# One full reading of x in another order of tiles, and four constants loaded through another queue

## The chip, the core and the metric

The kernel runs on one core of one Trainium2 chip. Its engines work side by side, each on its own list of instructions in order: TensorE (PE, with its weight loads as PEld), VectorE (DVE), ScalarE (ACT), GpSimd (POOL) and SyncE (SP). SP, ACT and POOL also issue DMA transfers, which sixteen DMA engines carry out between HBM and the chip's memory (SBUF). An instruction starts when those ahead of it on its engine have started and the semaphores that it waits for have been raised. The metric is the device time of one execution in microseconds; lower is better.

## The reference, cut to what matters

Four layers are applied in turn to an image x of 256 x 256 pixels with 128 channels in float32, each in the form `x = x + layer(gn(x))`: an attention along the rows, a recurrence in the Fourier domain, a triangle product, and a 3 x 3 convolution. Each begins with a group norm over the whole image:

```python
def _gn(v, G=32, eps=1e-5):
    B_, H_, W_, C_ = v.shape
    g = v.reshape(B_, H_, W_, G, C_ // G)
    m = jnp.mean(g, axis=(1, 2, 4), keepdims=True)
    s = jnp.var(g, axis=(1, 2, 4), keepdims=True)
    return ((g - m) / jnp.sqrt(s + eps)).reshape(v.shape)

x = x + _L0_conv_ref(_gn(x), ...)
x = x + _L1_conv_ref(_gn(x), ...)
x = x + _L2_conv_ref(_gn(x), ...)
x = x + _L3_conv_ref(_gn(x), ...)
```

The mean and variance of x for the first group norm need a reading of all of x before the first layer can start. The change lies in that reading.

## The kernel before

**The reading of x.** `statistics` (L194) takes x as 32 tiles of 2048 pixels, each `[128, 2, 1024]` in float32, 1 MB, loaded by one DMA that SP issues (L236). Seven tiles, 0 to 6, are loaded into buffers of their own, `kept` (L349), because the pass that follows starts with them and so needn't read them again. The other 25 go through the three buffers of `xin` (L235): a load can be issued only when VectorE has read the tile that was in its buffer three loads earlier. The order of the tiles is written out in `order` (L229): first 7 to 31, last the kept ones.

For each half of a tile VectorE subtracts a shift, the values of the first pixel, into `xs` (L239, the line L217 of the profile); ScalarE squares it into `sqx` (L242, shown as L54); and TensorE adds up both over the pixels in `acc` (L225, shown as L60). `xs` has three buffers, and these three operations are kept in the order of the program.

**What runs beside it.** `constants` (L156) loads four tables of 64 KB through SP at the very start: `ident`, `cmat`, `omat` and `g4`. Then SP loads `row` and `shc`, the shift in two layouts, and from `row` TensorE and VectorE make `sh`. `attention_weights` (L271) loads weights through ScalarE's queue and prepares them with small operations on VectorE and TensorE; these stand in the engines' lists among the subtractions of the first tiles. One of its results passes through ScalarE (`terms`) before VectorE forms `tot`.

`kernel_rows` (L165) computes H, the rows of a spectrum that the second layer uses. It loads its taps `ka` through GpSimd's queue and its table `tu` through SP; then sixteen times, after tiles 4, 5, 7, 8 and so on up to 26 in order of reading, TensorE forms `ph` and ScalarE copies it into H (L188, shown as L178). After the eighth and after the sixteenth copy GpSimd's queue writes H to HBM in four DMAs of 224 KB (L191), each of 14 rows of 16 KB.

**What follows.** When `acc` is complete, VectorE copies it to `accs` (L256); a chain of small operations gives mean and variance, `group_affine` (L75) turns them into scale and shift with `g4`, and `centering` (L129) uses `cmat`. Then the first pass of the attention transposes tile by tile (`turn`, with `ident`), starting with the kept tiles, and loads tile 7 and on once more. SP's list holds, between the loads of the reading and those of this pass, 25 small loads of weights for later layers.

A Tile framework places the semaphores. The DMAs of SP and ACT share eight of them in turn, and GpSimd's eight others; a DMA whose semaphore is still awaited from an earlier transfer waits for that one. Where nothing pins an instruction, a scheduler decides its place on its engine.

The lines shown in the profile are those of the innermost statement, so `load` appears as L70, `mm` as L60 and `act` as L54.

Of the kernel before, what the change touches and what calls it, by code (L numbers as in the profile page):

```python
# [30 lines left out]
class Kernel:  # L31
# [33 lines left out]
        self.nc.sync.dma_start(t, src.rearrange("(c o) -> c o", o=1))  # L65
        return t

    def load(self, pool, src, name):
        t = pool.tile(list(src.shape), F32, name=name)
        self.nc.sync.dma_start(t, src)  # L70
        return t


# [81 lines left out]

    def constants(self, pool):  # L156
        nc = self.nc
        self.ident = self.load(pool, self.i["c_ident"], "ident")
        self.cmat = self.load(pool, self.i["c_center"], "cmat")
        self.omat = self.load(pool, self.i["c_mean"], "omat")  # L160
        self.g4 = self.load(pool, self.i["c_group4"], "g4")
        self.eps = pool.tile([P, 1], F32, name="eps")
        nc.vector.memset(self.eps, LN_EPS)

# [29 lines left out]
    def statistics(self, wp, weights, HD_, kept, src):  # L194

        nc, I = self.nc, self.i
        V = nc.vector
        x = I["x"].rearrange("b h w c -> (b h w) c")  # L200
        NM, KEPT = NPIX // 2048, len(kept)
        mv = wp.tile([P, 2], F32, name="mvx")
        with ExitStack() as c:
            sp = c.enter_context(self.pool(name="sp", bufs=1))
            io = c.enter_context(self.pool(name="p0", bufs=3))
            ps = c.enter_context(self.pool(name="p0s", bufs=1, space=PSUM))
            row = sp.tile([1, P], F32, name="row")
            nc.sync.dma_start(row, x[0:1])
            shc = self.column(sp, x[0:1].rearrange("o c -> (o c)"), "shc")
            ones = sp.tile([P, P], F32, name="ones0")  # L210
            V.memset(ones, 1.0)
            psh = ps.tile([P, 4, P], F32, name="psh", tag="ph", bufs=2)
            self.mm(psh[:, 0], ones[0:1], row)
            sh = sp.tile([P, P], F32, name="sh")
            V.tensor_copy(sh, psh[:, 0])
            acc = ps.tile([P, 512], F32, name="acc")
            pin = lambda f: lambda *a, **k: self.tc.keep_in_program_order(f(*a, **k))  # L217
            last, count = None, [0, 0]

            def add_up(*pair):  # L220
                for h in range(2):
                    for j, t in enumerate(pair):
                        if t is not None:
                            o = 64 * j + 32 * h
                            pin(self.mm)(acc[o:o + 32], ones[:, :32], t[:, h * 512:(h + 1) * 512],  # L225
                                    start=count[j] < 2, stop=count[j] >= 4 * NM - 2)
                            count[j] += 1

            order = list(range(KEPT, NM)) + list(range(KEPT))  # L229
            spectrum, made = None, 0  # L230
            for n, m in enumerate(order):
                if m < KEPT:
                    xin = kept[m]
                else:
                    xin = io.tile([P, 2, 1024], F32, name="xin", bufs=3)  # L235
                nc.sync.dma_start(xin, src(m))  # L236
                for b in range(2):
                    xs = io.tile([P, 1024], F32, name="xs")
                    pin(V.tensor_tensor)(xs.rearrange("p (t c) -> p t c", t=8), xin[:, b].rearrange("p (t c) -> p t c", t=8),  # L239
                                    sh.unsqueeze(1).to_broadcast([P, 8, P]), ALU.subtract)  # L240
                    sq = io.tile([P, 1024], F32, name="sqx")
                    pin(self.act)(sq, xs, AF.Square)  # L242

                    add_up(xs, last)
                    last = sq
                if n == 1:
                    spectrum = self.kernel_rows(sp, ps, HD_)
                    next(weights)
                elif n == 9:
                    weights = next(weights)  # L250
                elif n >= 4 and n % 3 and made < 16:
                    spectrum(made)
                    made += 1
            add_up(None, last)
            accs = sp.tile([P, 512], F32, name="accs")
            V.tensor_copy(accs, acc)  # L256
            sel = sp.tile([P, 2], F32, name="sel")
            V.memset(sel, 0.0)
            V.memset(sel[:64, 0:1], 1.0 / 32 / NPIX)
            V.memset(sel[64:, 1:2], 1.0 / 32 / NPIX)  # L260
            pm = ps.tile([P, 2], F32, name="pmx")
            for t in range(4):
                self.mm(pm, accs[:, t * P:(t + 1) * P], sel, start=t == 0, stop=t == 3)
            V.tensor_copy(mv, pm)
            e = sp.tile([P, 1], F32, name="ex")
            V.tensor_tensor(e, mv[:, 0:1], mv[:, 0:1], ALU.mult)
            V.tensor_tensor(mv[:, 1:2], mv[:, 1:2], e, ALU.subtract)
            V.tensor_tensor(mv[:, 0:1], mv[:, 0:1], shc, ALU.add)
        return mv, weights

    def attention_weights(self, wp):  # L271
# [4 lines left out]
        def load(src, name):  # L276
            t = wp.tile(list(src.shape), F32, name=name)
            nc.scalar.dma_start(t, src)
            return t

        lns, lnb = (load(I["L0_conv_ln_" + n].rearrange("(c o) -> c o", o=1), "ln" + n[0]) for n in ("scale", "bias"))
        w, wb, raws = {}, {}, {nm: load(I["L0_conv_W" + nm], "raw" + nm) for nm in "qkvgb"}
        wo = {"f": load(I["L0_conv_Wo"], "wo"), "h": wp.tile([P, P], F32, name="woh")}
        m32 = load(self.i["c_block32"], "m32")
        yield
# [1248 lines left out]
def arrays_of(inputs):  # L1534


    arrays = constants()
    for name, a in inputs.items():
        a = np.asarray(a)
        if name in _RENAMED:  # L1540
            if name == "L3_conv_kernel":
                a = a.reshape(9, P, P).transpose(2, 0, 1)
            else:
                a = a.T
            name = _RENAMED[name]
        arrays[name] = np.ascontiguousarray(a)


    taps = np.zeros((2, 3 * KS, HC, 32), np.float32)
    for n, m in enumerate("AB"):  # L1550
        re, im = (arrays.pop(f"L1_conv_{m}_{y}").transpose(1, 0, 2) for y in ("real", "imag"))
        for p0, q0, a in ((0, 0, re), (0, KS, im), (KS, 0, im), (2 * KS, KS, re)):
            taps[n, p0:p0 + KS, :, q0:q0 + KS] = a
    arrays["L1_taps"] = taps
    for g in "fid":
        arrays["L1_b" + g] = np.ascontiguousarray(np.tile(arrays.pop("L1_conv_b" + g).reshape(2, HC).T, (2, 1)))
    return arrays
# [16 lines left out]
```

## Time and profile before

| what | us |
|---|---|
| median of three runs | 5099.39 (5096.98 to 5099.84) |
| the profiled execution, its own time | 5096.92 |
| its span, first to last instruction | 5095.1 |
| TensorE busy in it | 4938.7 (97%) |
| first subtraction of the reading starts | 15.29 |
| last subtraction ends | 123.7 |
| `accs` copied out | 126.03 |
| first transposes of the pass that follows | 131.9 |

In a line of the timeline the first number is the start in microseconds from the start of the span, the second the time that it took, then engine, line, operation, what it writes and reads, and how many of them the line puts together. In brackets stands how long the engine was idle before it, and what released it. In a line of the windows stand the stretch, its length, then busy time of PE, PEld, DVE, ACT and POOL with their counts, the granted clock of TensorE, the busy share of the DMA engines and the GB/s that they moved. In a line of the queues stand packets, MB and the share of the time of 16 DMA engines; q1 is that of SP, q0 that of GpSimd.

### The profile page before, as it was taken

Reading aid. Unit: us, or ns where it says so; the run is one execution under the profiler, and the core shown is the slowest. Engines: PE = TensorE matmul, PEld = TensorE weight load, DVE = VectorE, ACT = ScalarE, POOL = GpSimd, SP = SyncE. Lnnn points to the kernel's source line nnn. Section 1 sums busy time; section 2 is a strip of 40 time slices with the busy share of each in tenths; the row PEclk is TensorE's granted clock in tenths of the full one; section 3 lists DMA queues with packets and bytes.
Section 4 is the critical chain, followed back from the end, with each engine's and each line's share of the span. In section 5 each row is a group of like instructions: output and inputs, shape, how many; then the busy total and the mean of one; then the engine's idle time right before and its main releaser. Section 6 shows DMA issues by size and latency. Waiting matters only on the chain. (4 is left out here: it accounts for less than half of the span.)

```text
span 5095.1 us, 78580 instructions
## 1 busy us (share of the span) xinstructions
PE 4938.7 (97%) x31357; PEld 2699.4 (53%) x31357; DVE 4100.7 (80%) x4797; ACT 3497.2 (69%) x4948; POOL 406.9 (8%) x592
## 2 busy tenths in 40 slices
PE   8999999999999899999999999899999999989999
PEld 2444555555555333333333333229999953349999
DVE  6666999999999799999999999775333537779886
ACT  6445888888888899999999999453333357762110
POOL 0331000000000000000000000240111010000000
PEclk9999999999999899999999999999999999999999
DMA  8894222222222222222222221588666778865432
GB/s 289 291 338 173 88 84 80 88 81 82 84 81 82 65 70 66 74 64 76 64 74 66 72 68 61 215 324 308 235 230 243 252 286 321 322 230 181 141 122 67
DMA packets 204461, 781.66 MB, mean 153 GB/s; under 512 B 56278, under 2 KB 59628, under 8 KB 154788
## 3 DMA queue, kind: packets, MB, share of 16 engines
q1 hardware_dynamic: 146638, 505.57, 29.6%
q0 software_dynamic: 56160, 270.64, 14.7%
q8 instruction: 250, 4.10, 0.3%
q14 instruction: 117, 0.96, 0.1%
q10 hardware_dynamic: 1296, 0.40, 0.0%
HBM read 505.18 MB, written 271.32 MB: 152 GB/s over the span
## 5 line engine op out<-in xcount | busy, mean ns | idle before, releaser
L565 DVE TENSOR_TENSOR e<-sc,bT 128x1024 f32<-128x1024 f32 x512 | 603.1, 1220 | 51.3 <-PE sc L60 50.4
L54 ACT ACTIVATE e<-e 128x1024 f32<-128x1024 f32 x512 | 540.3, 1055 | 63.1 <-DVE e L565 53.9
L1066 DVE TENSOR_TENSOR LR<-z,sg 128x512 f32<-128x512 f32 x256 | 268.6, 1049 | 363.5 <-ACT sg L54 363.5
L60 PE MATMUL m<-U,v 128*128 128x128 f32 x4608 | 516.9, 276 | 6.7 <-DVE v L1413 6.7
L60 PEld LDWEIGHTS m<-U,v 128*128 128x128 f32 x4608 | 516.8, 193 | 6.7 <-DVE v L1413 6.7
L60 PEld LDWEIGHTS z<-wf,zt 128*128 128x128 f32 x4096 | 460.0, 193 | 2.9 <-DVE zn L1066 2.7
L60 PE MATMUL z<-wf,zt 128*128 128x128 f32 x4096 | 460.2, 276 | 1.3 <-DVE zn L1066 1.3
L54 ACT ACTIVATE sg<-z 128x512 f32<-128x512 f32 x256 | 153.0, 597 | 308.8 <-PE z L60 308.8
L54 ACT ACTIVATE sq<-zs 128x1024 f32<-128x1024 f32 x192 | 202.4, 1054 | 196.3 <-DVE zs L374 156.9
L565 DVE TENSOR_TENSOR ks<-e 128x1024 f32<-128x1024 f32 x256 | 300.9, 1217 | 0.0
L60 PE MATMUL sc<-tq,tk 32*128 32x256 f32 x4096 | 297.7, 402 | 3.2 <-DVE e L565 2.3
L60 PEld LDWEIGHTS sc<-tq,tk 32*128 32x128 f32 x4096 | 186.9, 185 | 160.5 <-issue 97.1
L60 PE MATMUL nd<-e,tv 128*32 128x256 f32 x4096 | 271.7, 383 | 0.0
L54 ACT ACTIVATE dn<-dn 128x512 f32<-128x512 f32 x384 | 241.7, 629 | 14.2 <-DVE dn L565 3.4
L60 PE MATMUL av<-y,ident 128*128 128x512 f32 x384 | 191.3, 607 | 44.8 <-DVE y L903 44.8
L60 PE MATMUL po<-LR 128*128 128x256 f32 x1024 | 222.2, 380 | 7.0 <-DVE LR L1066 7.0
L1450 ACT COPY m4s<-m 128x512 f32<-128x512 f32 x32 | 18.7, 585 | 286.1 <-PE m L60 286.1
L60 PEld LDWEIGHTS po<-LR 128*128 128x128 f32 x1024 | 194.1, 190 | 34.2 <-DVE LR L1066 7.7
L60 PE MATMUL bx<-p,ident 128*128 128x512 f32 x384 | 193.3, 612 | 0.0
L54 ACT ACTIVATE o<-po 128x256 f32<-128x256 f32 x256 | 84.3, 381 | 145.3 <-issue 109.4
L60 PEld LDWEIGHTS nd<-e,tv 128*32 128x32 f32 x4096 | 120.2, 110 | 108.9 <-issue 42.9
L54 ACT ACTIVATE xp<-xr,ab 128x1536 f32<-128x1536 f32 (+1 forms) x48 | 76.9, 1653 | 137.6 <-DVE tf L1425 126.7
(364 smaller groups left out, 10354.7 us busy)
## 6 DMA issues: line engine op xcount, KB each, us to landing
zt<-znT SPq DMA_DIRECT2D x128, 1024.0 KB
znT<-zn POOLq DMA_DIRECT2D x64, 1024.0 KB, 5.2
xin<-x2T SPq DMA_DIRECT2D x64, 1024.0 KB
xin<-in_x_dram SPq DMA_DIRECT2D x50, 1024.0 KB
xr<-x3T SPq DMA_DIRECT2D x46, 768.0 KB
xT<-xo POOLq DMA_DIRECT2D x32, 1024.0 KB, 9.4
xr<-xT SPq DMA_DIRECT2D x64, 512.0 KB
zn<-znT SPq DMA_DIRECT2D x64, 512.0 KB
```

The lines of the kernel that those rows point to most:

```text
L54: return self.nc.scalar.activation(out, in_, func, bias=bias, scale=scale, **kw)
L60: return self.nc.tensor.matmul(out, lhsT, rhs, start=start, stop=stop)
L565: pin = lambda f: lambda *a, **k: tc.keep_in_program_order(f(*a, **k))
L1066: pin = lambda f: lambda *a, **k: tc.keep_in_program_order(f(*a, **k))
L1450: nc.scalar.copy(m4, m[4])
```

## The change

The reading takes the tiles in the order of their numbers, so the seven kept tiles come first and the 25 that go through `xin` after them. The four constants are loaded through GpSimd's queue instead of SP's, ahead of the taps.

```diff
-    def load(self, pool, src, name):
+    def load(self, pool, src, name, queue=None):
         t = pool.tile(list(src.shape), F32, name=name)
-        self.nc.sync.dma_start(t, src)
+        (queue or self.nc.sync).dma_start(t, src)
         return t
...
-        self.ident = self.load(pool, self.i["c_ident"], "ident")
-        self.cmat = self.load(pool, self.i["c_center"], "cmat")
-        self.omat = self.load(pool, self.i["c_mean"], "omat")
-        self.g4 = self.load(pool, self.i["c_group4"], "g4")
+        self.ident = self.load(pool, self.i["c_ident"], queue=nc.gpsimd, name="ident")
+        self.cmat = self.load(pool, self.i["c_center"], queue=nc.gpsimd, name="cmat")
+        self.omat = self.load(pool, self.i["c_mean"], queue=nc.gpsimd, name="omat")
+        self.g4 = self.load(pool, self.i["c_group4"], queue=nc.gpsimd, name="g4")
...
-            order = list(range(KEPT, NM)) + list(range(KEPT))
+
             spectrum, made = None, 0
-            for n, m in enumerate(order):
+            for n in range(NM):
+                m = n
                 if m < KEPT:
                     xin = kept[m]
                 else:
```

In the built program the order of instructions differs only in this stage. On SP, `row` and `shc` come first, then the loads of the seven kept tiles (with `tu` after the second), then those of the 25 others. On GpSimd the four constants stand ahead of the taps. On VectorE `sh` is made first, and the preparation of the weights is spread among the subtractions of the first six tiles. On TensorE and ScalarE the same operations stand in a slightly different order in the first tiles.

## The prediction

> **What bounds the kernel now.** I first read the whole span, then the stage that the diff touches, then what waits for what inside it.
>
> ```profile
> span 5095.1 us, 78580 instructions
> PE 4938.7 (97%) x31357; PEld 2699.4 (53%) x31357; DVE 4100.7 (80%) x4797; ACT 3497.2 (69%) x4948; POOL 406.9 (8%) x592
> ```
>
> TensorE is busy nearly everywhere, so a change in the first stage moves all later work as a block: what the stage gains or loses is the whole effect. The reading of x (L236) ends where `accs` is copied out, at 126.03 us. That is 2.5% of the span. The copies of the weight table and the first transposes follow by 132 us.
>
> The pace of that stage is in the timeline of ScalarE:
>
> ```profile
> 58.49 1.03 ACT L178 COPY H<-ph 128x512 f32<-128x512 f32 x1 [1.23 <-PE ph L60]
> ...
> 68.53 1.02 ACT L178 COPY H<-ph 128x512 f32<-128x512 f32 x1 [1.23 <-PE ph L60]
> ...
> 74.47 1.04 ACT L178 COPY H<-ph 128x512 f32<-128x512 f32 x1 [1.23 <-PE ph L60]
> ...
> 78.54 1.02 ACT L178 COPY H<-ph 128x512 f32<-128x512 f32 x1 [1.23 <-PE ph L60]
> ...
> 89.63 1.06 ACT L178 COPY H<-ph 128x512 f32<-128x512 f32 x1 [2.40 <-PE ph L60]
> ...
> 113.74 1.02 ACT L178 COPY H<-ph 128x512 f32<-128x512 f32 x1 [1.23 <-PE ph L60]
> 114.56 10.31 ACT L54 ACTIVATE sqx<-xs 128x1024 f32<-128x1024 f32 x10
> ```
>
> Every three tiles bring two copies of H, and the same one of the two comes back after 10.03 us (58.49, 68.53, 78.54): 3.34 us a tile, set by ScalarE's squares, its copies and its two waits for PE. Once in the stage the beat breaks: the successor of 74.47 was due at 84.5 and comes at 89.63. After 113.74 there are no more copies, and a tile takes about 2.35 us. VectorE's timeline says why it breaks, and when the stage starts and ends:
>
> ```profile
> 15.29 2.35 DVE L217 TENSOR_TENSOR xs<-xin,sh 128x1024 f32<-128x1024 f32 x2
> ...
> 24.76 2.36 DVE L217 TENSOR_TENSOR xs<-xin,sh 128x1024 f32<-128x1024 f32 x2 [0.34 <-PE ptot L533]
> ...
> 27.59 4.61 DVE L217 TENSOR_TENSOR xs<-xin,sh 128x1024 f32<-128x1024 f32 x4
> ...
> 76.40 1.23 DVE L217 TENSOR_TENSOR xs<-xin,sh 128x1024 f32<-128x1024 f32 x1 [1.28 <-ACT sqx L54]
> 83.72 2.36 DVE L217 TENSOR_TENSOR xs<-xin,sh 128x1024 f32<-128x1024 f32 x2 [6.09 <-DMA xin<-in_x_dram]
> ...
> 111.59 2.40 DVE L217 TENSOR_TENSOR xs<-kept,sh 128x1024 f32<-128x1024 f32 x2 [1.29 <-ACT sqx L54]
> 115.64 8.08 DVE L217 TENSOR_TENSOR xs<-kept,sh 128x1024 f32<-128x1024 f32 x7 [1.65 <-ACT sqx L54]
> 126.03 0.69 DVE L256 COPY accs<-acc 128x512 f32<-128x512 f32 x1 [2.30 <-PE acc L60]
> ```
>
> The 6.09 us wait at 83.72 is for a tile of x. Just before it POOL has written H to HBM (first of two times):
>
> ```profile
> 69.84 2.00 POOL L191 DMA_DIRECT2D HD<-H  x4 [67.31 <-ACT H L178]
> 115.05 2.00 POOL L191 DMA_DIRECT2D HD<-H  x4 [43.20 <-ACT H L178]
> ```
>
> The queues of 66 to 90 us and the windows show the price of that write:
>
> ```profile
> q1 hardware_dynamic: 1561, 6.05, 68.5%
> q0 software_dynamic: 128, 0.92, 22.7%
> ```
>
> ```profile
> 100.00:114.00 14.00, 13.47 (x116) 3.21 (x112) 9.78 (x9) 10.31 (x12) 0.00 (x0) 1.00 1.02 409
> 72.00:82.00 10.00, 9.18 (x78) 2.01 (x70) 4.34 (x4) 6.89 (x8) 0.00 (x0) 1.00 0.97 243
> ```
>
> The write moves 0.92 MB for 22.7% of 24 us on 16 engines, 95 us of engine time per MB; reads of x cost 43.5. While it runs (72 to 82 us) all queues together move 2.43 MB, so x gets 1.51 MB, 1.44 tiles in 10 us; undisturbed (100 to 114 us, 409 GB/s) a tile of 1.05 MB takes 2.56 us. **The second write starts at 115.05, in the last tiles.** There it hurts nobody today: those are the kept tiles, each with a buffer of its own, and SP has issued all seven by 100 us.
>
> **What the Trainium skill says.** "DMA: Bandwidth & Descriptors", section "Queues, rings and completion order": each DMA engine goes round-robin among the queues that have work, packet by packet, so H and x share the same engines; the 243 against 409 GB/s agrees. The same page, "Why a DMA increments its semaphore by 16 and not by 1": the engine count divides the slowest dimension, so H's 14 rows would go to 14 engines in few large pieces; the dear engine time above fits, the split itself no view shows. "Anatomy of one DMA — SWDGE (gpsimd) path": about 2.0 us fixed and bytes/436e3, so about 4.4 us for one tile alone (an estimate from the page). I use 5 us from issue to use: the wait at 36.00 and the like (0.2 to 1.3 us) in the three-buffer loop allow that little slack. "TensorE: Matmul & The Clock Gate", Part 1, gives a half clock after an idle window; the 0.50 windows at 28 and 132 us agree.
>
> **The change part by part.**
>
> (1) Constants to GpSimd's queue. SP loses four issues of 0.40 to 0.43 us, POOL gains four of about 0.6 (its taps' issues take 0.62). SP's first tile is now issued third, near 2 us instead of 5.41, since it also no longer waits for lanes that the constants held. POOL's taps come 4 x 0.6 = 2.4 us later; they are first read near 30 us, nothing. `ident` is first read by VectorE near 13 us and `cmat`, `g4` after 128 us: nothing, unless ident took over 10 us.
>
> (2) Tiles 0 to 6 first. Ten buffers (seven kept, three of `xin`) take loads without waiting for VectorE. Today SP's fourth tile waits until 17.67 for VectorE, and in 16 to 18 us the DMA moves only 35 GB/s. In the built program the first subtraction now stands just behind `grq`, where nine small operations preceded it after `wo` landed: today `woh` at 12.47, `xs` at 15.29, 2.8 us. And the fifth tile's subtraction stands ahead of `tot`, which covers today's 2.22 us wait for ScalarE's `terms`. If `wo` lands at 11 to 13 us (12.4 today; it is issued earlier, against more traffic), the five first tiles, with their 17 us of VectorE work less the 0.9 us put behind them, end at 27.5 to 29.5 instead of 32.2: a gain of 2.7 to 4.7. I take 3.5; the bounds are 0 (weights come late by what was won) and 6.
>
> (3) The middle. From the sixth tile on ScalarE paces, so the lead of the loads isn't cashed: nothing. At the first write of H the tile that comes late (the 20th) can't be issued before the 17th's buffer is free (71.7 us), with or without a lead; the write is on by 71.9. So the 5.1 us of the broken beat (89.63 less 84.5) stay. I take 0.3 gained; bounds 0 and 5.
>
> (4) The end. The last tiles go through three buffers: tile n+3 is issued when VectorE has done with n. In today's clock, the 30th tile (of 32) is issued at 109.1 and is in time; the 31st when the 28th is done, at 112.8; its transfer starts near 114.5, behind the 30th, and has some 0.4 tile left when the write of H takes hold near 116. The 32nd is issued when the 29th is done, at 116.9. So 1.4 tiles pass beside the write at 1.44 tiles in 10 us: until about 125.6, and 1.2 more until it is seen, 126.8. Its two subtractions end at 129.2; today VectorE ends at 123.7. Loss 5.5; bounds 1 (the write starts late enough for the 31st to pass) and 8.
>
> (5) Behind the stage. SP's 25 loads of later weights and the loads of tile 7 on come some 10 us later; tile 7 is transposed from 195 us on, and today its load is issued at 134.69, so 55 us cover it. The pass after has a beat of 9.54 us of PE with and without loads of x: nothing.
>
> Sum: -3.5 - 0.3 + 5.5 = +1.7 us. The profiled execution took 5096.92 (span 5095.1 and 1.8 around it), so 5098.6 by that clock; it lies 2.5 under the median of 5099.39, which gives 5101 for the median.
>
> **The rivals.** *The last loads escape the write of H*: for it, only 0.4 tile of the 31st stands in its way; against it, the 32nd can't be issued earlier. Then the end costs 1 to 2 us and the change nets -2: 5097. *The early lead covers the first write too*: head -6 and the 5.1 us of the broken beat gone, end at 1: about -10, 5089. Against it, the buffer rule in (3). *Slower, crowded head*: the tiles of x, from 2 us on, share the engines with the six weight loads of 64 KB on ScalarE's queue, for which VectorE waits in order before it subtracts anything. Price: 8 packets of each on an engine, each behind a packet of x (4 KB at 43.5 us per MB, 0.18 us), 1.4 us a load, six in a row 8.6. Then the first subtraction comes near 21 instead of 15.29 and with the end's 5.5 the sum is about +11: 5111. It decides once `wo` lands after about 18 us. For it: today rawq takes 4.1 us and wo 5.2, which is such sharing already; against it, the weights are issued earlier as well. *Nothing moves*: the pace is ScalarE's, head and end both hide: 5099.
>
> **How the numbers follow.** Main case 0.62; loads escape 0.16; nothing moves 0.07; both stalls gone 0.05; crowded head 0.10. 0.2% is 10 us, about what this measurement can tell from no change. Main, escape and nothing stay within it (0.85, and 0.01 from the edge of the others), the fourth is faster (0.04), the fifth slower. Range: the main case is +1.7 with -4 to +6 from its bounds; with part of the others 5095 to 5108.
>
> **What would show it.** Right: first subtraction near 12 us and the fifth tile done by 29; a wait of some 5 us for `xin` still in the middle; at the end waits of VectorE for `xin` of 5 us together, where today it has none; `accs` near 127.5. Wrong: `wo` after 18 us; no wait for `xin` in the last ten microseconds of the reading; a shift that arises after 140 us.

## The result, and the profile after

| | before | after |
|---|---|---|
| median of 20 runs each, us | 5098.59 (5093.95 to 5100.64) | 5103.61 (5101.17 to 5110.10) |
| ratio, 95% interval | | 1.0014 [1.0008, 1.0020] |
| the profiled execution, its own time | 5096.92 | 5101.69 |
| its span | 5095.1 | 5099.5 |
| first subtraction starts | 15.29 | 13.84 |
| first copy of H | 34.41 | 31.77 |
| last copy of H | 113.74 | 111.19 |
| `accs` copied out | 126.03 | 132.08 |

The changed kernel is slower by some 0.14%, which its interval tells from nothing, and which lies within the 0.2% that the forecast called no change. The stage of the reading is 6.05 us longer in the profile. The table splits it: 2.64 us are won before the first copy of H; at the last copy 2.55 of them are left, so the middle gave back 0.09; and between the last copy and `accs` the kernel before took 12.29 us, the changed one 20.89. This last difference, 8.6 us, is called *the end* below; it is worked out for each kernel as `accs` less the last copy of H less 12.29.

VectorE's timeline of the changed kernel shows the head, the break in the middle and the end:

```profile
13.84 2.35 DVE L217 TENSOR_TENSOR xs<-kept,sh 128x1024 f32<-128x1024 f32 x2
...
26.72 2.36 DVE L217 TENSOR_TENSOR xs<-kept,sh 128x1024 f32<-128x1024 f32 x2
...
81.16 2.36 DVE L217 TENSOR_TENSOR xs<-xin,sh 128x1024 f32<-128x1024 f32 x2 [6.17 <-DMA xin<-in_x_dram]
...
113.10 5.81 DVE L217 TENSOR_TENSOR xs<-xin,sh 128x1024 f32<-128x1024 f32 x5 [1.65 <-ACT sqx L54]
126.63 2.36 DVE L217 TENSOR_TENSOR xs<-xin,sh 128x1024 f32<-128x1024 f32 x2 [7.72 <-DMA xin<-in_x_dram]
132.08 0.69 DVE L257 COPY accs<-acc 128x512 f32<-128x512 f32 x1 [3.09 <-PE acc L60]
```

The fifth tile ends at 29.08 (before: 32.2). The wait for x in the middle is as long as before (6.17, before 6.09). New is the wait of 7.72 us in front of the last tile, the two subtractions at 126.63; none of the five halves of tiles just ahead of it, in the line of 113.10, waited for x.

ScalarE's timeline shows that the beat is otherwise the old one:

```profile
65.87 1.02 ACT L178 COPY H<-ph 128x512 f32<-128x512 f32 x1 [1.23 <-PE ph L60]
71.81 1.02 ACT L178 COPY H<-ph 128x512 f32<-128x512 f32 x1 [1.23 <-PE ph L60]
75.85 1.02 ACT L178 COPY H<-ph 128x512 f32<-128x512 f32 x1 [1.23 <-PE ph L60]
87.07 1.05 ACT L178 COPY H<-ph 128x512 f32<-128x512 f32 x1 [2.40 <-PE ph L60]
...
111.19 1.02 ACT L178 COPY H<-ph 128x512 f32<-128x512 f32 x1 [1.23 <-PE ph L60]
112.01 8.05 ACT L54 ACTIVATE sqx<-xs 128x1024 f32<-128x1024 f32 x8
127.95 2.19 ACT L54 ACTIVATE sqx<-xs 128x1024 f32<-128x1024 f32 x2 [7.89 <-DVE xs L217]
```

65.87 to 75.85 is the beat of 10 us; the successor of 71.81 was due at 81.83 and comes at 87.07, 5.2 us late (before 5.1). Then ScalarE idles 7.89 us in front of the last tile, as VectorE did. What the last tile meets is in the timelines of POOL and of SP (the line of 114.35 is the last of the 25 loads through `xin`) and in the windows of the changed kernel, one in the first write of H and one in the second:

```profile
67.18 1.98 POOL L191 DMA_DIRECT2D HD<-H  x4 [62.52 <-ACT H L178]
112.50 1.98 POOL L191 DMA_DIRECT2D HD<-H  x4 [43.34 <-ACT H L178]
```

```profile
114.35 0.37 SPq L237 DMA_DIRECT2D xin<-in_x_dram  x1
114.77 1.67 SPq L70 DMA_DIRECT2D rwf<-in_L_conv_Wf_dram  x1
```

```profile
69.00:79.00 10.00, 9.52 (x78) 2.15 (x72) 4.68 (x5) 7.21 (x8) 0.16 (x1) 1.00 0.95 242
114.60:124.60 10.00, 5.38 (x46) 1.06 (x38) 4.31 (x4) 5.31 (x6) 0.00 (x0) 0.96 0.80 183
```

SP issues its last load of x at 114.35; POOL has issued the write of H just before, and the first packets of the write run at 114.47. By the trace's records of single packets, the 256 packets of the last tile run from 116.40 to 126.12: 9.7 us for one tile, where the tile ahead of it took 3.5 (111.38 to 114.90).

### The profile page after: what moved, and what is told of

It is laid out like the page before. It is cut to its first block, busy times and chain, and to the rows that moved or that the text cites. A ratio compares the mean times of both kernels' runs of the same rounds, so it can differ in the third digit from the quotient of the medians.

```text
span 5099.5 us, 78579 instructions
## 1 busy us (share of the span) xinstructions
PE 4941.0 (97%) x31357; PEld 2699.2 (53%) x31357; DVE 4100.1 (80%) x4797; ACT 3496.7 (69%) x4948; POOL 409.2 (8%) x596
```

## The experiments

Each ratio is against the kernel before, run beside it on the same chip. The last column but one is the time in which the packets of the last tile of the order ran, from the trace's DMA records.

| run | median, us (before beside it) | ratio, 95% | last copy of H | last tile's packets, us | the end, us |
|---|---|---|---|---|---|
| constants alone | 5097.43 (5098.95) | 0.9995 [0.9987, 1.0004] | 112.40 | kept tile, early | 0.0 |
| order alone | 5111.13 (5098.95) | 1.0022 [1.0013, 1.0031] | 115.24 | 10.6 | 8.6 |
| second write behind | 5101.10 (5098.95) | 1.0007 [0.9998, 1.0015] | 110.72 | 4.9 | 2.4 |
| both writes behind | 5092.96 (5098.95) | 0.9988 [0.9981, 0.9995] | 105.97 | 6.5 | 5.9 |
| four kept first, three last | 5097.10 (5097.70) | 0.9998 [0.9989, 1.0006] | 113.32 | kept tile, early | 0.0 |
| old order, both behind | 5093.60 (5097.70) | 0.9991 [0.9982, 0.9999] | 107.30 | kept tile, early | 0.0 |
| small pieces | 5096.24 (5097.70) | 0.9998 [0.9989, 1.0006] | 106.59 | 6.3 | 6.4 |
| changed, once more | 5110.45, one run (5097.70) | | 113.30 | 10.3 | 8.6 |
| behind the weights too | 5097.33 (5096.25) | 1.0003 [0.9994, 1.0011] | 105.59 | 4.1 | 1.1 |
| old order, small pieces | 5088.41 (5096.25) | 0.9986 [0.9979, 0.9993] | 106.43 | kept tile, early | 0.0 |
| four buffers | 5094.70 (5096.25) | 0.9994 [0.9985, 1.0003] | 106.06 | 3.6 | 0.0 |

Two cautions go with the table. Sizes were missed more often than signs: `accs` came 1 to 2 us later than expected with the constants alone, with the order alone, with four kept tiles first and three last, and in the old order with both writes behind; 2 us later in the changed kernel once more; and 3 to 5 us later with both writes behind in the changed order. And the median doesn't follow `accs` closely. With both writes behind, `accs` is 1.84 us ahead of the kernel before and the median 5.99 under it; with four buffers `accs` is 7.68 ahead and the median 1.55 under. These two differences are not explained, so what a run says of the reading is read from its timeline.

### The two parts of the change, each alone

The changed kernel with the old order (the constants alone stay moved):

```diff
-            for n in range(NM):
-                m = n
+            order = list(range(KEPT, NM)) + list(range(KEPT))
+            for n, m in enumerate(order):
```

> The kernel before with the constants on GpSimd's queue and the order of the tiles as it was. Theory (the gain at the head comes from this part, through the order that the scheduler then gives VectorE, and the loss at the end from the order of the tiles): first subtraction near 13.8 us as in the changed kernel, the first copy of H near 31.8 instead of 34.41, the break of 5 us in the middle unchanged, no wait of VectorE for x in the last five tiles, accs near 123.5 us; time 2 to 3 us under the kernel before. Rival (the head is gained by loading seven tiles ahead): first subtraction and first copy of H as in the kernel before, accs near 126.

And the changed kernel with the constants on SP again (the order alone stays changed):

```diff
-        self.ident = self.load(pool, self.i["c_ident"], queue=nc.gpsimd, name="ident")
+        self.ident = self.load(pool, self.i["c_ident"], "ident")
...
```

> The changed order of the tiles with the constants on SP's queue as they were. Theory: the head as in the kernel before (first copy of H near 34.4), the wait of some 7.7 us for the last tile as in the changed kernel, so accs near 134.5 us, 2.5 later than in the changed kernel; time 7 to 9 us over the kernel before. Rival (seven tiles ahead make the head): first copy of H near 31.8, accs near 132.

VectorE's timeline of the first, with the constants moved:

```profile
13.64 2.35 DVE L217 TENSOR_TENSOR xs<-xin,sh 128x1024 f32<-128x1024 f32 x2
...
26.96 2.36 DVE L217 TENSOR_TENSOR xs<-xin,sh 128x1024 f32<-128x1024 f32 x2
29.24 0.15 DVE L531 TENSOR_REDUCE tot<-terms 128x1 f32<-128x8 f32 x1
...
124.69 0.69 DVE L256 COPY accs<-acc 128x512 f32<-128x512 f32 x1 [2.30 <-PE acc L60]
```

and of the second, with the order changed:

```profile
15.40 2.35 DVE L217 TENSOR_TENSOR xs<-kept,sh 128x1024 f32<-128x1024 f32 x2
18.65 2.35 DVE L217 TENSOR_TENSOR xs<-kept,sh 128x1024 f32<-128x1024 f32 x2
25.12 0.16 DVE L532 TENSOR_REDUCE tot<-terms 128x1 f32<-128x8 f32 x1 [2.97 <-ACT terms L54]
...
130.72 2.36 DVE L217 TENSOR_TENSOR xs<-xin,sh 128x1024 f32<-128x1024 f32 x2 [7.77 <-DMA xin<-in_x_dram]
136.13 0.69 DVE L257 COPY accs<-acc 128x512 f32<-128x512 f32 x1 [3.05 <-PE acc L60]
```

The head belongs to the constants: its first subtraction is at 13.64 with them moved, and at 15.40 with the order alone, where the first copy of H is even 0.84 us later than before (35.25 against 34.41). The reason stands in the order of VectorE's list: with the constants moved, `tot` comes behind the fifth tile's subtractions and waits for nothing; with them on SP it comes ahead of the third tile and the engine waits 2.97 us for ScalarE. No earlier start is to be seen just ahead of it: `woh`, which needs the weight `wo`, starts at 12.74 with the constants moved and at 12.58 without. VectorE's list alone was not varied, so the reason is argued; the attribution is not: over all profiles of this case the first copy of H comes at 31.43 to 33.15 in the eleven with the constants moved, in whichever order of tiles, and at 34.41 and 35.25 in the two with them on SP. Seven tiles without a wait for a buffer win nothing that can be seen at the head. Of its 2.40 us (32.01 against 34.41) the run with the constants alone has 1.34 left at the last copy of H; there the beat is broken by 5.9 instead of 5.1 us. Two executions of the changed kernel differ too (5.2, and 5.7 in its run at the end); why is open. The end belongs to the order alone: 8.6 us with it, nothing without it.

### The end: what passes beside the last tile

The changed kernel, with the second write of H issued by SP behind all loads of x:

```diff
+        self.behind = []
...
-                    nc.gpsimd.dma_start(HD_[n, :, k], H[n][32 * k:32 * k + 2 * KS])
+                    if n == 1:
+                        self.behind.append((HD_[n, :, k], H[n][32 * k:32 * k + 2 * KS]))
+                    else:
+                        nc.gpsimd.dma_start(HD_[n, :, k], H[n][32 * k:32 * k + 2 * KS])
...
+            for dst, t in self.behind:
+                nc.sync.dma_start(dst, t)
             add_up(None, last)
             accs = sp.tile([P, 512], F32, name="accs")
```

> The changed kernel with the second write of H issued by SP behind all loads of x instead of by GpSimd as soon as H is ready. Theory (the end is lost because the last tile shares the DMA engines with this write): the 7.7 us wait of VectorE falls to at most 2, accs near 124 to 126 instead of 132.1, time 6 to 8 us under the changed kernel, give or take 3 for the clock at later stages. Rival (three buffers alone make the last tiles late): the wait stays over 5 us, accs over 130.

With both writes behind (`if True` in place of `if n == 1`):

> The changed kernel with both writes of H issued by SP behind all loads of x. Theory: also the 5.2 us break of ScalarE's beat after the eighth copy of H goes, accs near 119 to 121, time 11 to 13 us under the changed kernel and 6 to 8 under the kernel before. Rival (the break comes from the three buffers or from HBM and not from the write): accs as in the run with the second write alone moved. If the eight writes hold up what follows (loads of the next pass, buffers that lie where H was), the first transposes come later than 6 us after accs.

And with both of them behind the 25 loads of later weights as well, which are then issued within the reading's function (against the run with both behind):

```diff
+            self.later_weights(later)
             for dst, t in self.behind:
                 nc.sync.dma_start(dst, t)
             add_up(None, last)
...
-                if m == 5:
-                    self.later_weights(later)
-                elif m == 12:
+                if m == 12:
...
```

> The changed kernel, but H is written to HBM only after the reading: all eight DMAs stand on SP's queue behind the last load of x and behind the 25 small loads of later weights. Nothing but x then passes in the last ten microseconds. Theory (of the 8.6 us by which the end of the changed kernel is later, the write of H beside the last tile makes about 6, the three buffers alone about 2.4): no broken beat, last copy of H at 105.5 to 107, and accs 12.3 + 2 to 3 us behind it; waits of VectorE for x in the last ten microseconds of 2 to 3 us together. Rival (three buffers make the end paced by the loads once the beat has no break, whatever H does): accs 12.3 + 5.5 to 6.5 us behind the last copy of H, as in the run with both writes right behind the last load.

VectorE's timelines of the three, in this order:

```profile
117.83 2.36 DVE L221 TENSOR_TENSOR xs<-xin,sh 128x1024 f32<-128x1024 f32 x2 [1.66 <-DMA xin<-in_x_dram]
120.71 2.36 DVE L221 TENSOR_TENSOR xs<-xin,sh 128x1024 f32<-128x1024 f32 x2 [0.52 <-DMA xin<-in_x_dram]
125.37 0.69 DVE L263 COPY accs<-acc 128x512 f32<-128x512 f32 x1 [2.30 <-PE acc L60]
```

```profile
118.11 2.36 DVE L221 TENSOR_TENSOR xs<-xin,sh 128x1024 f32<-128x1024 f32 x2 [2.98 <-DMA xin<-in_x_dram]
124.19 0.69 DVE L263 COPY accs<-acc 128x512 f32<-128x512 f32 x1 [3.71 <-PE acc L60]
```

```profile
114.35 2.36 DVE L221 TENSOR_TENSOR xs<-xin,sh 128x1024 f32<-128x1024 f32 x2 [1.03 <-DMA xin<-in_x_dram]
119.01 0.69 DVE L264 COPY accs<-acc 128x512 f32<-128x512 f32 x1 [2.30 <-PE acc L60]
```

To be issued behind the last load on the same queue doesn't keep a write from running beside it: in the second of the three SP issues the writes from 110.43, right behind the last load, and the packets of that load run for 6.5 us. With the weights between them the packets take 4.1 us and the wait in front of the last tile is 1.03. So, by difference, 7.5 of the 8.6 us are owed to the write beside the last tile, and 1.1 to three buffers with nothing but the small loads of weights beside. The third kernel also has no break in the middle; the first keeps the break and its end is 2.4, so the break is not what makes the end long. Over all these runs the end grows, by and large, with the time of the last tile's packets. The 2 to 3 us expected for the buffers were too much, and the rival's 5.5 to 6.5 is out.

With both writes away from the middle the beat isn't broken (last copy of H at 105.97 and 105.59). Yet the third kernel is no faster than before in its time: the 7.0 us that it is ahead at `accs` are gone by 145 us, because the next pass writes `xo` where H lies, and now waits until H has been read out. VectorE's timeline of the third kernel shows it:

```profile
132.42 1.23 DVE L382 COPY xo<-pt 128x1024 f32<-128x1024 f32 x1 [7.89 <-DMA HD<-H]
```

### One more buffer, and other orders

The changed kernel with six kept tiles and four buffers of `xin`, the same memory; the next pass then loads tile 6 once more:

```diff
-                    xin = io.tile([P, 2, 1024], F32, name="xin", bufs=3)
+                    xin = io.tile([P, 2, 1024], F32, name="xin", bufs=4)
...
-            kept = [kp.tile([P, 2, 1024], F32, name=f"kept{m}") for m in range(7)]
+            kept = [kp.tile([P, 2, 1024], F32, name=f"kept{m}") for m in range(6)]
...
-            for m in range(7, 9):
+            for m in range(6, 8):
```

> The changed kernel with six kept tiles instead of seven and four buffers of xin instead of three (the same memory), so the last tile is issued one tile earlier, about 3 us before the second write of H; the attention pass loads tile 6 once more in exchange. Theory (the end is late because the last tile is issued just when H takes the engines): accs 12.3 + 0 to 2 us behind the last copy of H instead of 12.3 + 8.6, time 6 to 9 us under the changed kernel at the end of the reading. Rival (the three buffers only hide that the loads have fallen behind since the first write of H): still 5 us or more late. The broken beat in the middle: theory 1 to 3 us smaller, since one more tile lies ready; at least unchanged.

VectorE's timeline:

```profile
81.10 2.36 DVE L217 TENSOR_TENSOR xs<-xin,sh 128x1024 f32<-128x1024 f32 x2 [2.00 <-DMA xin<-in_x_dram]
...
107.96 8.08 DVE L217 TENSOR_TENSOR xs<-xin,sh 128x1024 f32<-128x1024 f32 x7 [1.65 <-ACT sqx L54]
118.35 0.69 DVE L257 COPY accs<-acc 128x512 f32<-128x512 f32 x1 [2.30 <-PE acc L60]
```

Both losses are gone. The end is 0.0: POOL issues the second write of H from 107.37, its first packets run at 109.85, and by then the last tile's packets (106.54 to 110.13) are nearly through. And the wait in the middle falls from 6.17 to 2.00, which the beat absorbs (75.97 to 85.99, 10.02 us). That the middle vanished whole was more than expected. `accs` is 7.68 us ahead of before, and the profiled span is 6.9 us shorter; the median, 1.55 us under before with runs of 5084.29 to 5096.69, doesn't tell the kernel from before.

The changed kernel with the kept tiles split, four first and three last:

```diff
-                m = n
+                m = n if n < 4 else n + 3 if n < NM - 3 else n - (NM - 7)
```

> The changed kernel with four kept tiles read first, the other 25 in the middle and three kept tiles last. Theory (only the last tiles, loaded through three buffers beside the second write of H, lose): head as in the changed kernel (first copy of H near 31.8), break in the middle of about 5 us, no long wait for x in the last tiles because the three kept ones have buffers of their own, accs near 123.5 us, 2.5 under the kernel before; time 1 to 4 us under the kernel before. Rival (the loss at the end is a matter of the write alone, whichever buffer the tile goes to): a wait of over 5 us for one of the last tiles, accs near 130.

The end is 0.0 and the middle keeps its wait (5.87 us). Three tiles with buffers of their own at the end are enough to cover the second write.

### The middle: the write itself

The old order with the constants moved and both writes behind (the edits of the first and of the fourth kernel together):

> The old order of the tiles, constants on GpSimd's queue, both writes of H issued by SP behind all loads of x. Theory: head 2.4 earlier, the break in the middle gone (5.2), the kept tiles at the end landed in time, so accs near 118.5 us, 7.5 under the kernel before, and the time 5 to 9 us under it. Rival (the loop of three buffers is then paced by the DMA, as the waits of 2 to 3 us of the run with both writes moved hint): accs over 121.

No break, no end; `accs` at 119.59, 6.44 us ahead. The other way to free the middle is to leave the writes in their places and cut their rows of 16 KB to 4 KB:

```diff
-                    nc.gpsimd.dma_start(HD_[n, :, k], H[n][32 * k:32 * k + 2 * KS])
+                    for u in range(0, N, 64):
+                        nc.gpsimd.dma_start(HD_[n, :, k, u:u + 64], H[n][32 * k:32 * k + 2 * KS, u:u + 64])
```

In the changed kernel:

> The changed kernel with each write of H cut into four DMAs with rows of 4 KB instead of 16 KB, still on GpSimd's queue at the same place. Theory (x is starved because each packet of H is four times as long as one of x on the same engine): with equal packets x gets about half of the engines, the break in the middle falls from 5.2 us to under 3 and the last wait from 7.7 to under 4, accs near 126 to 128. Rival (the write to HBM or its rows on 14 engines are dear whatever the packet): both waits within 1 us of the changed kernel's.

In the old order, with the constants moved:

> The kernel before with the constants on GpSimd's queue and its own order of tiles, H written at its two times on GpSimd's queue but in pieces of 4 KB rows. Theory (the two losses are separate: the pieces of 16 KB break the beat, the order of tiles makes the late end): last copy of H at 106.5 to 107.5, accs 12.3 us behind it at 118.5 to 120, time 5 to 8 us under the kernel before. Rival (the pieces of 4 KB cost the loads of x as much in all, spread over the stage): accs at 124 or later, time within 2 us of the kernel before.

Of the second, the windows and the queues from 66 to 90 us, the stretches that the prediction read in the kernel before, and ScalarE's timeline:

```profile
72.00:82.00 10.00, 9.64 (x84) 2.31 (x80) 6.77 (x6) 7.56 (x8) 3.58 (x8) 1.00 0.96 369
```

```profile
q1 hardware_dynamic: 1855, 7.14, 82.3%
q0 software_dynamic: 512, 0.92, 12.5%
```

```profile
76.35 1.04 ACT L178 COPY H<-ph 128x512 f32<-128x512 f32 x1 [1.23 <-PE ph L60]
...
86.35 1.07 ACT L178 COPY H<-ph 128x512 f32<-128x512 f32 x1 [1.23 <-PE ph L60]
```

The same 0.92 MB of H now costs 12.5% of 24 us on 16 engines, 52 us of engine time per MB instead of 95, and all queues together move 369 GB/s where they moved 243. The beat isn't broken (76.35 to 86.35) and the end is 0.0, `accs` at 118.72. Cutting the rows changes two things, though: they are shorter, and POOL now issues sixteen DMAs instead of four, so that the write's packets run for 12.4 us (69.64 to 82.01) instead of 9.2. Which of the two frees the beat was not separated. This kernel has the lowest ratio here, 0.9986 [0.9979, 0.9993], some 7 us under the kernel before and, by the two ratios, some 14 under the changed one, and it does without the new order; its interval doesn't tell it from the two kernels with both writes behind. In the changed order the small pieces free the middle alike, but not the end (6.4 us, with the last tile's packets running for 6.3 us beside the write), as VectorE's timeline shows:

```profile
119.57 2.36 DVE L218 TENSOR_TENSOR xs<-xin,sh 128x1024 f32<-128x1024 f32 x2 [2.34 <-DMA xin<-in_x_dram]
125.28 0.69 DVE L258 COPY accs<-acc 128x512 f32<-128x512 f32 x1 [3.35 <-PE acc L60]
```

### The changed kernel once more

> The changed kernel once more, one look. Theory (the steps of 1 to 3 us in the shift against the kernel before that arise after 400 us come from where the half-clock windows of TensorE fall, which differs from one execution to the next): the reading as in the first profile (accs within 0.5 us of 132.1) and other steps at 440, 1700 and 3200 us, so a span that differs by some us. Rival (the steps belong to the change): the same steps at the same places.

This execution took 5110.45 us where the first profile of the same kernel took 5101.69. VectorE's timeline has the same end, later by the 2.1 us that head and middle took longer:

```profile
128.52 2.36 DVE L217 TENSOR_TENSOR xs<-xin,sh 128x1024 f32<-128x1024 f32 x2 [7.50 <-DMA xin<-in_x_dram]
134.14 0.69 DVE L257 COPY accs<-acc 128x512 f32<-128x512 f32 x1 [3.26 <-PE acc L60]
```

The other 6.6 us come later. Set side by side instruction by instruction, the two executions part by 3.6 us near 1700 and by 3.3 after 4100; in both places a stretch at half clock lies differently. The windows of 4130 to 4175 us, of the first profile and then of this one, show the second:

```profile
4130.00:4175.00 45.00, 40.73 (x142) 18.30 (x144) 22.95 (x33) 30.74 (x37) 2.71 (x5) 1.00 0.89 350
```

```profile
4130.00:4175.00 45.00, 40.73 (x140) 20.84 (x139) 16.84 (x26) 25.37 (x36) 3.78 (x7) 0.92 0.74 288
```

The granted clock is 0.92 instead of 1.00: 6.8 us at half clock, 3.4 of full clock lost, of which 3.0 reach the time of what follows. Such steps come in executions of one and the same kernel. They may be why the twenty runs of the changed kernel fall into 5101 to 5104 (twelve) and 5107 to 5110 (eight), but only these two executions were compared. Whether the new timing makes the steps more frequent is open.

## Why the prediction was right, and where its steps were not

The forecast was no change within 0.2%, at 5101; the median is 5103.61, within the range. The sum over the reading was +1.7 and is +6.05; the median moved by +5.0. That a sum missed by 4.35 us still lies in the range is in part luck: 0.2% is 10 us, wide against what a stage of 126 us can shift, and 1.5 of the 6.05 us were given back behind the stage in the profile. What was right is the account of the parts: head, middle and end each came within about 3 us of what was taken for them, though the cause given for the head was wrong.

**(1) Constants.** Booked at nothing, for what it might cost: no cost of it was seen, `ident` and the taps kept nobody waiting. But it is this part that wins the head.

**(2) The head.** 3.5 was taken, and 3.1 measured at the end of the fifth tile (29.08, in the interval named) or 2.64 at the first copy of H, inside the bounds of 0 to 6. In the second execution of the same kernel it is 2.1 and 1.64, with the fifth tile at 30.07, just outside the interval. The cause was wrong. The step described the new order of VectorE's list, which does the work (`xs` soon behind `grq`, the fifth tile ahead of `tot`), and credited it, with ten buffers that need no wait, to the order of the tiles. The two runs with one part each show that the list changes with the constants, and that the early tiles win nothing to be seen. The first subtraction came at 13.84, not near 12.

**(3) The middle.** Right: the break stays, 5.2 us, and 0.1 is given back instead of 0.3 won (1.2 in the second execution). The reason, that three buffers bind whatever lead there is, is shown by the run with four: its wait falls to 2.00 and the beat holds.

**(4) The end.** The mechanism is right and its size failed: 5.5 taken, 8.6 measured, above the bound of 8. In the clock of before (2.55 us added to that of after) the last tile was issued at 116.9, as forecast. The 31st wasn't late at all: its packets were through by 114.90 in the changed kernel's clock, just after the write's first at 114.47. The term at fault is the rate beside the write, 1.44 tiles in 10 us from the first write. It was one tile in 9.7 us, 1.03 in 10; all queues moved 183 GB/s there, not 242. So the last tile was seen at 129.2 instead of 126.8 in the same clock, 2.4 us more, and the last sums added 0.8 (3.09 us from the last subtraction to `accs`, before 2.30): TensorE had fallen to half clock from 123.8 to 130.7 us while it waited.

The trace of before held the right figure. There SP issues the load of the 20th tile just as the packets of the first write begin, at 71.86:

```profile
71.70 0.37 SPq L236 DMA_DIRECT2D xin<-in_x_dram  x1
```

VectorE reads that tile at 83.72, 12.0 us from issue to use. The last tile of the changed kernel took 12.3 (114.35 to 126.63), and 12.1 in the second execution. 116.9 and 12.0 make 128.9, close to the 129.2 seen. The 1.51 MB that x got beside the first write belonged to several tiles in flight, and their mean rate says too little of how long one of them takes. The small loads of weights behind the last tile have no match in the middle; without a write, the last tile took 4.1 us beside such loads, and what they add beside the write was not tried.

The 5 us from issue to use without a write were a little short. The fit behind the prediction's 4.4 us is for DMAs of GpSimd's path, while x comes through SP; in the run with the weights between, the last tile took 5.6 (108.76 to 114.35).

**(5) Behind the stage.** Right in its place: the shift of 6.05 at `accs` is 5.44 from 140 to 400 us and 4.53 at the end of the span. Between, it moves by steps of about 3 us both ways where half clock falls differently, a term that the prediction didn't have and that is larger than its whole sum of 1.7.

Of the rivals, the escape of the last loads and the crowded head didn't come: `woh`, which needs `wo`, starts at 12.94 without a wait. That an early lead covers the first write too is refuted for three buffers.

## What to carry to other kernels

Before an order of loads is turned round, ask which tiles stand last and what else passes then: tiles with buffers of their own at the end absorb a burst that a short ring of buffers cannot, and one more buffer was worth more at `accs` than the seven tiles of lead. When a load will start beside such a burst, look in the trace for a single load that did so already, and take its time from issue to use; a mean rate over several loads in flight says too little. A burst of writes with large rows can be mended at the write, by smaller pieces; moved behind all loads of the stage, it held up the next user of its memory for 7.9 us. And where a change has two parts, run each alone, since a scheduler may let one part bring what was meant of the other.

## What the hardware showed that wasn't expected

At the first write, rows of 16 KB from GpSimd's queue took 95 us of engine time per MB, the same bytes in rows of 4 KB 52, near the 44 of the loads of x beside them (7.14 MB in 82.3%). The queue is not the reason: in the run with both writes behind, SP's queue carried the rows of 16 KB, and a packet of 16 KB took 1.55 us, 94 us per MB. Nor is 52 a constant of the small rows: at the second write in the old order with small pieces, with hardly any load of x left beside it, they took 40.8% of 14 us (108 to 122), 99 us per MB. Why is open.

The Trainium skill ("DMA: Bandwidth & Descriptors", section "Queues, rings and completion order") tells that an engine takes its queues in turn by packets; the runs agree insofar as small pieces of H leave x 3.0 MB in the 10 us from 72 us on and large ones 1.5, but they don't show the turns themselves.

The half clock came in stretches of 3.4 us and its multiples up to 20.5, but for the one that the end of the span cuts off, as with the free-running window of 3413 ns in the Trainium skill, "TensorE: Matmul & The Clock Gate", Part 1, section "What's actually happening". One of 6.8 us, between 4133 and 4154 us, cost about 3 us in six of the thirteen profiles and was absent in the others. Two single executions of the changed kernel differed by 8.8 us, 6.6 of them outside the reading: a difference of 5 us between two single executions is thus no evidence on a stage; its own timeline is.
